# One written order for the keys' stage and cross-attention, ACT's too, with queries two units ahead throughout and feed-forward tiles between the last two units' work

## The chip, the cores and the metric

The kernel runs on one core of a Trainium2 chip. The core has a matrix engine (TensorE, PE in the profile, with its weight loads as PEld), a vector engine (VectorE, DVE), an activation engine (ScalarE, ACT), GpSimd (POOL) and a queue that issues most transfers (SyncE, SP). The metric is the device time of one execution in microseconds; lower is better. All arithmetic is in float32.

## What is computed

One decoder layer for 32 sequences of 64 tokens (2048 tokens) of width 512. `x` is replaced three times:

```python
x = _layernorm(x + _L0_attn_ref(x, ...))      # 32 heads of 128, 8 key heads, 512 cached keys + 64 new ones
x = _layernorm(x + _L0_xattn_ref(x, ctx_4096, Wq, bq, Wkv, bkv, Wo, bo))
x = _layernorm(x + _L0_ffn_ref(x, W, b, A, B, p_scores))

# cross-attention: 32 heads in 8 groups of 4; every sequence has 64 context rows of its own
q = (query @ Wq + bq);  k_, v_ = split(kv @ Wkv + bkv)
o = softmax(q k^T / sqrt(128)) v;   return o @ Wo + bo

# feed-forward: a full product and one of low rank (8 x 16), clamped by their norms
z = x W^T + b;  m = sum_e p_e (x A_e) B_e
return z + min(0.5 |z| / (|m| + 1e-6), 1) * m
```

## The kernel before

Tokens are handled in four blocks of 512 (tb 0 to 3), each of four tiles of 128 rows. `acc[tb]` holds a block's running x, rows on partitions. Large products are done by Strassen and Winograd's scheme with seven products in place of eight: each needs sums of its operands beforehand (by GpSimd mostly), and after each product its PSUM bank is read by VectorE or ACT and added up. Queries are done so on two levels (`DeepQueries`): sets s = 0 and s = 1, each with products 1 to 7. Few banks are at hand, so TensorE waits at a product whose bank has not been read yet.

There are four stages.

- **Self-attention**, to about 1820 us. The diff does not touch it.
- **The keys' stage** (`with ExitStack() as st`, L1244 to L1339): keys and values of the context, 15 pairs (gp, tb) of seven products each, the 16th having been done earlier (`KV_ORDER` 1, 6, 5, 7, 2, 4, 3; "step" counts them from pair (0, 1) on). Product 1 and 2 go to a bank that ACT reads (L591, L592), the others to banks that VectorE reads (L595). Between the products a table, `fill`, places other work at given steps: the first layernorm of blocks 1, 2, 3, 0. Of each block it places the statistics (`stats`, bn_stats on VectorE and a square root on ACT), the scaling by ACT (`scale_by_act`, L190: reciprocal and shift on VectorE, four pieces on ACT), four turns (`turn_rows`, L150) and 16 small transfers on SP (`move_rows`, L155) that together transpose the block, then `token_parts` (L1203): the operand sums of the block's tokens, which are stored to `tl_all` for all later queries. These sums are made by `deep_parts` (L413): ACT copies four inner blocks, r11, r21, r12 and r22, and GpSimd makes the sums; r12 is overwritten by GpSimd before ACT copies it.
- **Cross-attention** in 32 units n = (g, tb), g the key group. In the loop (L1572 to L1711), unit n does: `attend(n-1)` (weights by values, then `output_sums` on GpSimd into `sox`), `scores(n)`, the softmax of n (`largest`, `exponentials`, `denominators`, `weights`, `turn`, `move`), the queries of a later unit m (14 products), and the output product of unit n-1 (seven products `w`, added to `acc`). `prep` is the preparation of the next group's weights (`weight_parts`, on GpSimd), done after `q_sums` of units with m % 4 = 3. m is n + 2 up to n = 25; at n = 26 there are no queries (`SKIP`), from 27 to 30 m is n + 1, and 31 has none. As a block's last unit ends, its second layernorm is made (`projected`), with turns and moves into xT for blocks 0 and 1, and TensorE transposes for blocks 2 and 3.
- **Feed-forward** (`feed_forward`, L1503) of each block: `pu` (x by A), and for each tile `pz` (x by W) and `pm`. Blocks 0 and 1 come within the last units; blocks 2 and 3 after them.

What sets the order: a scheduler orders the instructions of each engine, except where an engine is put under `tc.manual_schedule`; then its instructions run in the order in which the program writes them. Before, the keys' stage has PE, DVE and Pool written and ACT by the scheduler; units 0 to 30 have PE, Pool, DVE and ACT written; from unit 31 on only PE and Pool. The queues (SP's above all) issue in the order they are given. In the trace each engine runs its instructions one behind the other, so a waiting instruction holds all that stand behind it.

```python
for k, tb in enumerate((1, 2, 3, 0)):
    stats, scale = layernorm_parts(tb, "a", by_act=True)
    i = place(17 * k, stats, True)
    i = place(i + 1, scale) + 1
    for j in range(TPB):
        i = place(i, lambda tb=tb, j=j: turn_rows(acc[tb][:, j, :], room, j))
    fill[i - 1].append(lambda: move_rows(room, raw0))
    fill.setdefault(i + 5, []).append(lambda tb=tb: all_parts(token_parts(tb, raw0)))
```

Of the kernel before, what the change touches and what calls it, by code (L numbers as in the profile page):

```python
# [16 lines left out]
P = 128  # L17
DIM = 512
# [34 lines left out]
def decoder_layer(  # L53
# [115 lines left out]
    def layernorm_parts(tb, name, by_act=False):  # L169
# [20 lines left out]
        def scale_by_act():  # L190
            nc.vector.reciprocal(rstd, rstd)
            shift = small.tile([P, TPB], F32, tag="shift", name=f"shift_{name}_{tb}")
            nc.vector.scalar_tensor_tensor(shift, mv[:, :, 0], -1.0, rstd, ALU.mult, ALU.mult)
            for j in range(TPB):
                nc.scalar.activation(
                    a[:, j, :], a[:, j, :], AF.Identity, bias=shift[:, j : j + 1],
                    scale=rstd[:, j : j + 1],
                )

        return stats, scale_by_act if by_act else scale  # L200
# [105 lines left out]
    def output_sums(o, name, fourth_last=True):  # L306

        a = {(i, j): o[j][:, :, i * HF : (i + 1) * HF] for i in range(2) for j in range(2)}
        t = {i: big.tile([P, 2, HF], F32, tag=f"so{i}", name=f"{name}_{i}") for i in range(1, 5)}
# [860 lines left out]
    with ExitStack() as ph:  # L1170
# [72 lines left out]

        with ExitStack() as st:  # L1244
            ke = st.enter_context(tc.tile_pool(name="ke", bufs=1))
            psum.append(st.enter_context(tc.tile_pool(name="kps", bufs=1, space=PSUM)))
            st.enter_context(tc.manual_schedule(engines={
                mybir.EngineType.PE, mybir.EngineType.DVE, mybir.EngineType.Pool
            }))
# [21 lines left out]
            fill = {}  # L1271
# [8 lines left out]
            for k, tb in enumerate((1, 2, 3, 0)):  # L1280
                stats, scale = layernorm_parts(tb, "a", by_act=True)
                i = place(17 * k, stats, True)
                i = place(i + 1, scale) + 1
                for j in range(TPB):
                    i = place(i, lambda tb=tb, j=j: turn_rows(acc[tb][:, j, :], room, j))
                fill[i - 1].append(lambda: move_rows(room, raw0))
                fill.setdefault(i + 5, []).append(
                    lambda tb=tb: all_parts(token_parts(tb, raw0))
                )
                for j in (0, 2):  # L1290
                    while i in fill:
                        i += 1
                    fill[i] = [lambda tb=tb, j=j: add_bias(tb, j)]

            def queries(n, p):
# [3 lines left out]
                for s in range(2):  # L1299
                    for group in ((1, 5), (6, 2), (7,), (3, 4)):  # L1300
                        for i in group:
                            q.step(s, i)
                            q.read()
                        if i == 4:
                            run(q.post(s))
                            next_operands(n + 1, s)
                        yield
# [3 lines left out]
            for k, (gp, tb) in enumerate(pairs):  # L1311
# [6 lines left out]
                for i in KV_ORDER:  # L1318
# [4 lines left out]
                    run(fill.pop(step, []))  # L1323
                    step += 1
# [6 lines left out]
                if tb == NTB - 1 and gp == 2:  # L1331
                    load_xq(0, raw0)
                    all_parts(weight_parts(raw0))
# [4 lines left out]
            assert not fill  # L1338
            psum.pop()  # L1339

        sb = ph.enter_context(tc.tile_pool(name="xa", bufs=2))
        d_2 = sb.tile([P, 7, 4, P], F32, name="d_2", bufs=1)
# [28 lines left out]
        def exponentials(n, pr):  # L1371
# [3 lines left out]
            es[pr] = e = sb.tile(shape, F32, tag="e", name=f"ex{g}_{tb}_{pr}")  # L1375
# [39 lines left out]
        def attend(n):  # L1415

            g, tb = units[n]
            oTs[n] = output_tiles(f"oTx{g}_{tb}")
# [35 lines left out]
            left = output_sums(oTs.pop(n), f"sox{g}_{tb}", False)  # L1454
# [4 lines left out]
        def projected(n):  # L1459
            g, tb = units[n]  # L1460
            del pjs[n]
            if g == NKV - 1:
                stats, scale = layernorm_parts(tb, "x", by_act=True)
                due.append(stats)
                scales.append(scale)
                xT.append((raw, wqs.rearrange(flat)[:, : NC * TB].rearrange(
                    "p (c n) -> p c n", c=NC), rooms[:, 0, :, :], rooms[:, 1, :, :])[tb])
                if tb < 2:
                    later.append(lambda: turn_block(tb))
                else:  # L1470
                    later.append(lambda: transpose_block(tb, "x2", FREE))

        def turn_block(tb):
            room = sb.tile([P, DIM // SQ, SQ, TPB], F32, tag="room", name=f"room2_{tb}", bufs=1)
            for j in range(TPB):
                turns.append(lambda j=j: turn_rows(acc[tb][:, j, :], room, j))
            turns.append(lambda: move_rows(room, xT[tb]))

        def a_turn():

            if turns:
                turns.pop(0)()
                if len(turns) == 1:
                    turns.pop(0)()

# [17 lines left out]
        def feed_forward(tb, between=None):  # L1503
# [3 lines left out]
            pu = sc.tile([P, TB], F32, tag="sc", name=f"pu{tb}")  # L1507
# [6 lines left out]
            for i in range(TPB):  # L1514
                if between and i == TPB - 1:
                    between()
# [4 lines left out]
                pz = bank([P, DIM], f"pz{u}", (("qx", "qz") * 2 if tb < 2 else FREE)[i])  # L1521
                pm = (sc.tile([P, DIM], F32, tag="sc", name=f"pm{u}") if tb < 2 or i % 2 else
                      bank([P, DIM], f"pm{u}", ("qy", "wz")[i // 2]))
                for c in range(NC):
# [3 lines left out]
                    if c == (NC - 1 if i == 0 else 1):  # L1528
# [18 lines left out]
        FREE = ("qx", "qz", "wx", "wy")  # L1547
        ffn_w, turns = [], []
        N = len(units)
        load_kv(0)  # L1550

        units_order = ExitStack()
        units_order.enter_context(tc.manual_schedule(engines={
            mybir.EngineType.PE, mybir.EngineType.Pool, mybir.EngineType.DVE,
            mybir.EngineType.Activation,
        }))


        def parts(n, *made):

            for part, pr in made:
                if n < N:
                    part(n, pr)

        due, prep, shifts = [], [], []
        mxs, es, dens, scales = {}, {}, {}, []

        LAST = N - 1  # L1570
        SKIP = N - NTB - 2
        for n in range(N + 1):  # L1572
            if n == LAST:

                units_order.close()
                ph.enter_context(tc.manual_schedule(
                    engines={mybir.EngineType.PE, mybir.EngineType.Pool}
                ))
            m = n + 2 if n < SKIP else n + 1 if SKIP < n < LAST else None
            if m:  # L1580
                qn = deep_queries(m, QS if n else [QS[0], {"x": "wx", "z": "wz", "w": "wy"}])

            def q_step(s, *products):
                for i in products if m else ():
# [3 lines left out]
            def q_sums(s):  # L1588
                if not m:
                    return  # L1590
                if s:
                    own = qn.post(s)
                    if m == n + 1:
                        shifts.extend(own)
                    run(shifts)
                    if m > n + 1:
                        shifts.extend(own)
# [6 lines left out]
            def w(i):  # L1604
                if n == 0:
                    return
                pj = pjs[n - 1]
                pj.step(i)
                pj.reads.pop(0)()
                if i == 4:  # L1610
                    projected(n - 1)

            def w_rest():
                if n:
                    pjs[n - 1].read()

            if n > 1:
                attend(n - 1)
            if n == N:
                run(scales)  # L1620
                run(later)
                feed_forward(1)
            elif n != 1:
                scores(n)
            parts(n, (largest, 0), (largest, 1))
            q_step(0, 1)
            if n == 0:
                load_xo(0)
                run(held)
            parts(n, (exponentials, 0), (exponentials, 1))  # L1630
            if n == LAST:
                load_ffn()
                norm = [*due, *scales, *later]
                due, scales, later = [], [], []
            if n == 0:
# [3 lines left out]
                parts(n, (weights, 0))  # L1639
                q_step(1, 1, 5)  # L1640
                parts(n, (weights, 1))
                q_step(0, 3, 4)
                q_sums(0)
                parts(n, (turn, 0), (turn, 1))
                move(n)
                q_step(1, 6, 2, 7)
# [4 lines left out]
            if m and m % NTB == NTB - 1 and m // NTB + 1 < NKV:  # L1651
# [5 lines left out]
            if not m:  # L1657
                run(shifts)
            if n == 1:
                attend(0)  # L1660
                q_step(0, 3, 4)
                q_sums(0)
                q_step(1, 1, 5)
                w(1)
                w_rest()
                q_step(1, 6)
            else:
                w(1)
                q_step(0, 3)
                w_rest()  # L1670
# [3 lines left out]
            parts(n, (weights, 1), (turn, 0))  # L1674
            w(2)
            parts(n, (turn, 1))
            if n < N:
                move(n)
            if n < LAST:
                run(due)  # L1680
            if n > 1:
                q_step(1, 6)
            q_step(1, 2, 7)
            w(6)
            q_step(1, 3, 4)
            q_sums(1)
            if n < LAST:
                run(scales)
                run(later)
            w(5)  # L1690
            a_turn()
            w(7)
            a_turn()
            w(3)
            a_turn()
            w(4)
            a_turn()
            if n < N and units[n][1] == 0:
                load_xo(units[n][0])
            if m and m % NTB == 0 and 1 < m // NTB + 1 < NKV:  # L1700
# [61 lines left out]
```

## Time and profile before

| what | value |
|---|---|
| median of 3 runs | 3049.51 us (3049.48 to 3049.62) |
| the profiled execution's own time | 3048.54 us |
| its span, first to last instruction | 3046.8 us |
| mean granted TensorE clock | 0.994 |
| TensorE busy | 2994.2 us, 16128 products |
| TensorE's gaps over 0.06 us, all | 41.9 us |
| of these before 100 us / 1780 to 2052 / 2052 to 2110 / from 2760 on | 8.2 / 7.5 / 5.8 / 19.9 us |

The profiled execution lies 0.97 us under the median, and 1.74 us of it lie around the span. The profile's page gives for each engine the busy time; a view of waits gives, for each engine, the idle time ahead of its instructions and what ended it ("PE qx_3x L479 <- ACT d_in L492" is a product into bank qx_3x by the instruction of line 479 that could start once ACT had finished the instruction of line 492 that writes d_in). A view of windows gives the busy time of each engine between two times and the clock that TensorE was granted (1.00 is full). A timeline gives instructions in order, with the wait ahead of each in brackets.

The stretches in which TensorE was granted half its clock begin at 2058.06 us (for 3.41 us), 2768.03 (6.83), 2884.09 (6.83), 2901.15 (3.41), 2948.94 (6.83), 2979.66 (3.41) and, after TensorE's last product, 3041.1 (7.68).

### The profile page before, as it was taken

The numbers are of one execution on the slowest core, as the hardware profiler recorded it, in microseconds if no ns is written. First come the engines' busy times: TensorE is split into PE (matmuls) and PEld (weight loads), VectorE is DVE, ScalarE is ACT, GpSimd is POOL, SyncE is SP. The second block draws the span as 40 slices with busy tenths as digits, with TensorE's granted clock in tenths as the row PEclk, the third lists the DMA queues.
The fourth block names the chain that finished last, engine by engine and source line by source line (L and its number), as shares of the span: only waits on it lengthen the run. The fifth ranks groups of instructions, "written<-read, shape, count | busy, mean of one in ns | idle before, by whom it ended". The sixth has DMA issues, their size and how long they took to land.

```text
span 3046.8 us, 46458 instructions
## 1 busy us (share of the span) xinstructions
PE 2994.2 (98%) x16128; PEld 2344.6 (77%) x16128; DVE 2130.9 (70%) x3905; ACT 1131.5 (37%) x2794; POOL 1218.1 (40%) x1024
## 2 busy tenths in 40 slices
PE   8999999999999999999999999999999999999988
PEld 6777777777777777777777768998999999998864
DVE  6787777877877877877877756535666656666665
ACT  4322232332233232232232232325555545545453
POOL 4221321321321322322322135647667657756531
PEclk9999999999999999999999999999999999999999
DMA  6454444444445445444444355655544545553421
GB/s 183 128 131 126 113 111 124 113 111 127 109 117 128 105 117 132 102 120 129 102 117 120 85 133 196 241 205 192 170 171 169 195 168 172 179 171 127 138 72 39
DMA packets 221785, 418.16 MB, mean 137 GB/s; under 512 B 48176, under 2 KB 102960, under 8 KB 212592
## 3 DMA queue, kind: packets, MB, share of 16 engines
q1 hardware_dynamic: 206464, 387.26, 44.2%
q0 software_dynamic: 4304, 19.01, 1.8%
q10 hardware_dynamic: 10784, 8.92, 1.0%
q8 instruction: 130, 2.13, 0.3%
q14 instruction: 103, 0.84, 0.1%
HBM read 207.12 MB, written 33.82 MB: 79 GB/s over the span
## 4 chain that ended last, share of the span: by engine, by line
PE 91%; DVE 4%; ACT 2%; SPq 1%; DMA 1%; issue 1%; POOL 1%; DVEq 0%; ACTq 0%; POOLq 0%
PE po L871 16%; PE s L820 16%; PE pox L1430 2%; PE sx L1360 2%; PE qx_0x L479 2%; PE qx_3x L479 2%; PE qx_1x L479 2%; PE qx_2x L479 2%; PE wx_1y L340 1%; PE w_1y L340 1%; PE q_3y L340 1%; PE w_0y L340 1%; PE q_2y L340 1%; PE w_3y L340 1%; PE q_0y L340 1%; PE q_1y L340 1%
## 5 line engine op out<-in xcount | busy, mean ns | idle before, releaser
L828 ACT ACTIVATE p<-s,nmax 128x576 f32<-128x576 f32 x512 | 379.0, 740 | 1210.1 <-DVE nmax L825 1165.3
L820 PE MATMUL s<-kT,qT 128*128 128x288 f32 x2048 | 574.7, 406 | 0.5 <-ACT p L828 0.5
L871 PE MATMUL po<-pT,v 128*128 128x512 f32 (+1 forms) x1280 | 548.9, 602 | 3.0 <-DMA pT<-T 2.4
L820 PEld LDWEIGHTS s<-kT,qT 128*128 128x128 f32 x2048 | 387.7, 190 | 100.6 <-issue 18.7
L825 DVE TENSOR_REDUCE nmax<-s 128x1 f32<-128x576 f32 x512 | 383.5, 749 | 59.5 <-PE s L820 58.7
L851 DVE STREAM_TRANSPOSE T<-p 128x576 f32<-128x576 f32 x512 | 393.9, 769 | 12.7 <-ACT p L841 7.4
L871 PEld LDWEIGHTS po<-pT,v 128*128 128x128 f32 (+1 forms) x1280 | 213.5, 189 | 202.5 <-issue 172.5
L843 DVE TENSOR_SCALAR p<-p,den 128x576 f32<-128x576 f32 x488 | 301.4, 618 | 17.1
L311 POOL TENSOR_TENSOR so<-oT,oT 128x512 f32<-128x512 f32 x32 | 40.7, 1271 | 545.3 <-ACT oT L894 545.2
L837 DVE RECIPROCAL den<-den 128x1 f32<-128x1 f32 x512 | 83.9, 164 | 224.8 <-ACT p L828 210.4
L314 POOL TENSOR_TENSOR so<-oT 128x512 f32<-128x512 f32 x32 | 40.7, 1270 | 310.3 <-PE w_1y L340 92.8
L1387 ACT ACTIVATE ex<-ex,denx 128x64 f32<-128x64 f32 x512 | 129.1, 338 | 2.8 <-DVE denx L1382 2.8
L1449 ACT ACTIVATE oTx<-pox,bv 128x128 f32<-128x128 f32 x256 | 73.4, 490 | 134.4 <-PE pox L1430 134.4
L236 POOL TENSOR_TENSOR tx<-xT 128x512 f32<-128x512 f32 x31 | 40.6, 1310 | 199.1 <-PE q_3z L340 63.3
L311 POOL TENSOR_TENSOR sox<-oTx,oTx 128x512 f32<-128x512 f32 x32 | 40.6, 1269 | 161.6 <-DVE oTx L1451 155.6
L521 POOL TENSOR_TENSOR qTx<-d_in 128x512 f32<-128x512 f32 x68 | 85.1, 1273 | 44.1 <-ACT d_in L497 42.8
L828 ACT ACTIVATION_READ_ACCUMULATOR p<-s,nmax 128x1 f32 x512 | 98.7, 193 | 0.0
L528 ACT ACTIVATE qTx<-qTx,bq 128x512 f32<-128x512 f32 x128 | 82.5, 713 | 15.0 <-POOL qTx L521 15.0
L521 POOL TENSOR_TENSOR qTx<-d 128x512 f32<-128x512 f32 x60 | 75.1, 1272 | 25.9 <-ACT d L497 24.5
L1451 DVE TENSOR_SCALAR oTx<-pox,bv 128x128 f32<-128x128 f32 x256 | 72.9, 423 | 14.1 <-PE pox L1430 14.0
L1360 PEld LDWEIGHTS sx<-kv_room,qTx 128*64 128x64 f32 x2048 | 62.5, 138 | 12.2 <-issue 9.9
L894 ACT COPY oT<-po 128x512 f32<-128x512 f32 x128 | 68.2, 587 | 4.3 <-PE po L871 3.8
(566 smaller groups left out, 6236.8 us busy)
## 6 DMA issues: line engine op xcount, KB each, us to landing
pT<-T SPq DMA_DIRECT2D x1016, 80.0 KB
pT<-T SPq DMA_DIRECT2D x1008, 64.0 KB
xT<-tl SPq DMA_DIRECT2D x31, 1792.0 KB
tlb<-tl SPq DMA_DIRECT2D x31, 1344.0 KB
xT<-in_xT SPq DMA_DIRECT2D x123, 256.0 KB
kv_room<-kv SPq DMA_DIRECT2D x33, 512.0 KB
pTx<-Tx SPq DMA_DIRECT2D x256, 64.0 KB
kv<-c SPq DMA_DIRECT2D x30, 512.0 KB
```

Of the source, the lines that this page charges most:

```text
L340: nc.tensor.matmul(self.banks[b][:, m, :], self.left[i][:, k, m * P : (m + 1) * P], self.right[i][:, k, :], start=(first and m + k == 0), ...
L479: nc.tensor.matmul(o[:, j, :], self.left[s][:, j, LEFT[i], :], self.right[s][:, j, RIGHT[i], :], start=(first and j == 0), stop=(j == len( ...
L521: nc.gpsimd.tensor_tensor(self.q[:, :, i, :, v, :], x.rearrange("p (o u) n -> p o u n", o=2), y.rearrange("p (o u) n -> p o u n", o=2), AL ...
L820: nc.tensor.matmul(s[:, a, :HALF], qTs[n // REP][:, units[n][2], i * P : (i + 1) * P], kTs[g][:, a * HALF : (a + 1) * HALF], start=True, s ...
L825: nc.vector.tensor_reduce(nmax, s[:, :, :HALF], AX.XY, ALU.max, negate=True)
L828: nc.scalar.activation(p.rearrange("q (a k) -> q a k", a=2), s[:, :, :HALF], AF.Exp, bias=nmax, accum_out=den,)
L837: nc.vector.reciprocal(den, den)
L843: nc.vector.tensor_scalar(p, p, den, None, ALU.mult)
L851: nc.vector.transpose(Ts[n][:, :, i, :], ps_.pop((n, i)).rearrange("q (b k) -> q b k", k=SQ))
L871: nc.tensor.matmul(pos[n].rearrange("d (a q) -> d a q", a=NQD), vs[units[n][0]][rows, v, :], pTs[n // 2][rows, :, chunk, :], skip_group_ch ...
L1360: nc.tensor.matmul(s[b * SEQ : (b + 1) * SEQ, i * REP + h, :], qTs[n][:, h, pr * HF + c0 : pr * HF + c0 + SEQ], kvs[n][:, pr, 0, c0 : c0 + ...
L1387: nc.scalar.activation(e[:, k, :], e[:, k, :], AF.Copy, scale=den[:, k : k + 1])
```

## The change

1. One manual order, `units_order`, covers PE, Pool, DVE and ACT from the start of the keys' stage to the end of unit 30 (before: the keys' stage had its own without ACT).
2. `layernorm_parts(..., by_act=True)` gives the scaling as a head (reciprocal and shift) and four pieces. In the keys' stage the head is placed at the step after the statistics, the pieces two by two at steps with remainder 2 or 5 by 7 (table `scaling`), each pair followed by its turns; `token_parts` at the first such step from seven after the last turn on.
3. The weights' preparation for unit 0 is placed at pair (3, 0), product 2, and shifts of the first queries wait in `shifts` and run at pair (3, 3), product 5, or in unit 0.
4. The exponentials have two fixed tiles in place of a rotating tag.
5. Queries: m is n + 2 in all units up to 29, none in 30. Units 0 and 1 are written anew; in unit 1 the sums of set 0 (and `prep`) come before `attend(0)`.
6. Units 29, 30 and what follows are written out: the statistics of block 0 after output product 4 in unit 29; its pieces, turns and moves in unit 30; then the feed-forward of block 0 with `attend(30)` before its last tile, the scores and softmax of 31, the feed-forward of block 1 with `attend(31)` before its last tile, the output products of 30 and 31 in the order 1, 5, 6, 3, 7, 2, 4, with block 2's transposes between those of 31, then blocks 2 and 3. `load_ffn` (the feed-forward's weights: three transfers on SP, nine on GpSimd) moves from unit 31 to unit 30.
7. The last unit's outputs and sums use `d_in` and `d_2`; the banks of the feed-forward are given as arguments, and `pm` follows the whole `pz` in the last tile of blocks 0 and 1 too.

```diff
+        def head():
             nc.vector.reciprocal(rstd, rstd)
             nc.vector.scalar_tensor_tensor(shift, mv[:, :, 0], -1.0, rstd, ALU.mult, ALU.mult)
+        def piece(j):
+            nc.scalar.activation(a[:, j, :], a[:, j, :], AF.Identity, ...)
...
+        units_order.enter_context(tc.manual_schedule(engines={PE, Pool, DVE, Activation}))
         with ExitStack() as st:
-            st.enter_context(tc.manual_schedule(engines={PE, DVE, Pool}))
...
             for k, tb in enumerate((1, 2, 3, 0)):
-                stats, scale = layernorm_parts(tb, "a", by_act=True)
+                stats, (head, *pieces) = layernorm_parts(tb, "a", by_act=True)
                 i = place(17 * k, stats, True)
-                i = place(i + 1, scale) + 1
-                for j in range(TPB):
-                    i = place(i, lambda tb=tb, j=j: turn_rows(acc[tb][:, j, :], room, j))
-                fill[i - 1].append(lambda: move_rows(room, raw0))
-                fill.setdefault(i + 5, []).append(lambda tb=tb: all_parts(token_parts(tb, raw0)))
+                i = place(i, head)
+                j = 0
+                while j < TPB:
+                    while i % 7 not in (2, 5):
+                        i += 1
+                    scaling.setdefault(i, []).extend(pieces[j : j + 2])
+                    for jj in (j, j + 1):
+                        last = place(i + 1 + jj - j, lambda tb=tb, j=jj: turn_rows(...)) - 1
+                    i, j = i + 1, j + 2
+                fill[last].append(lambda: move_rows(room, raw0))
+                i = last + 7
+                while i % 7 not in (2, 5):
+                    i += 1
+                scaling.setdefault(i, []).append(lambda tb=tb: all_parts(token_parts(tb, raw0)))
...
                         if i == 4:
-                            run(q.post(s))
+                            shifts.extend(q.post(s))
...
                     run(fill.pop(step, []))
+                    run(scaling.pop(step, []))
+                    if gp == 3 and tb == 3 and i == 5:
+                        run(shifts)
+                    if gp == 3 and tb == 0 and i == 2:
+                        run(first)
+                        run(second)
...
+            if n == 1:
+                q_step(0, 3, 4)
+                q_sums(0)
+                attend(0)
+                q_step(1, 1, 5, 6)
+                parts(n, (weights, 1), (turn, 0))
+                q_step(1, 2)
+                w(0, 1)
+                q_step(1, 7, 4)
+                parts(n, (turn, 1))
+                move(n)
+                q_step(1, 3)
+                q_sums(1)
+                w(0, 2, 6, 5, 7, 3, 4)
...
+                if n == LAST - 2:
+                    q_step(1, 6)
+                    w(n - 1, 6, 5, 7, 3, 4)
+                    norms[0][0]()
+                    q_step(1, 2, 7, 3, 4)
+                    q_sums(1)
...
+        n = LAST - 1
+        attend(n - 1)
+        load_ffn()
+        scores(n)
+        head, *pieces = norms[0][1]
+        head()
+        run(pieces)
+        parts(n, (largest, 0), (largest, 1))
+        w(n - 1, 1)
+        parts(n, (exponentials, 0), (exponentials, 1))
+        turns, moves = turn_parts(0)
+        run(turns, 2)
+        w(n - 1, 5)
+        run(turns)
+        moves()
+        parts(n, (denominators, 0), (denominators, 1))
+        w(n - 1, 6)
+        run(shifts)
+        parts(n, (weights, 0))
+        w(n - 1, 3)
+        parts(n, (weights, 1), (turn, 0))
+        w(n - 1, 7)
+        parts(n, (turn, 1))
+        move(n)
+        w(n - 1, 2, 4)
+        units_order.close()
...
+        norm(1, True)
+        feed_forward(0, "sc", ZT, ("sc", "sc", "sc", "qy"), {3: [lambda: attend(LAST - 1)]})
+        n = LAST
+        scores(n)
+        for part in (largest, exponentials, denominators, weights, turn):
+            parts(n, (part, 0), (part, 1))
+        move(n)
+        feed_forward(1, "wx", ZT, ("wy", "sc", "sc", "sc"), {3: [lambda: attend(LAST)]})
+        w(LAST - 1, 1, 5, 6, 3, 7, 2, 4)
+        norm(2, False)
+        turned = [transpose_tile(2, j, ("wx", "wy", "wz", "qz")[j]) for j in range(TPB)]
+        w(LAST, 1, 5, 6, 3, 7)
+        run(turned, 2)
+        w(LAST, 2)
+        run(turned)
+        w(LAST, 4)
+        norm(3, False)
+        feed_forward(2, "sc", ("wx", "wz", "wx", "wz"), ("sc",) * TPB, {
+            3: [transpose_tile(3, j, ("qx", "qz", "wy", "qy")[j]) for j in range(TPB)]
+        })
+        feed_forward(3, "sc", ("qx", "qz", "wx", "wz"), ("sc",) * TPB)
```

## The prediction

> **What bounds the kernel now.** I read the page first, then TensorE's waits by stage, then the stages' windows, then the timelines around the waits.
>
> ```profile
> PE 2994.2 (98%) x16128; PEld 2344.6 (77%) x16128; DVE 2130.9 (70%) x3905; ACT 1131.5 (37%) x2794; POOL 1218.1 (40%) x1024
> PE 91%; DVE 4%; ACT 2%; SPq 1%; DMA 1%; issue 1%; POOL 1%; DVEq 0%; ACTq 0%; POOLq 0%
> ```
>
> TensorE (PE) is busy 98% of the span and carries 91% of the chain that ended last. The change removes no product, so it can only move TensorE's idle gaps. The windows (start:end and length, then busy time of PE, PEld, DVE, ACT and POOL, the granted clock, the DMA share, GB/s) show where those are:
>
> ```profile
> 1840.00:2052.00 212.00, 206.38 (x1459) 193.97 (x1459) 109.11 (x163) 65.10 (x148) 116.99 (x99) 1.00 0.58 212
> 2052.00:2107.00 55.00, 49.22 (x479) 45.31 (x476) 30.69 (x60) 32.04 (x85) 40.53 (x33) 0.97 0.63 214
> 2107.00:2760.00 653.00, 653.00 (x5525) 596.62 (x5526) 405.39 (x756) 342.29 (x927) 441.54 (x357) 1.00 0.51 175
> ```
>
> Units 2 to 25 (2107 to 2760) have no gap at all. What can be won or lost lies in three places: the keys' stage (5.6 us of gaps), units 0 and 1 (5.8 us) and the tail from unit 26 on, whose waits are:
>
> ```profile
> PE qx_3x L479 <- ACT d_in L492: 4.0, 1, 4.0
> PE wx_1x L340 <- DVE acc L547: 3.6, 1, 3.6
> PE x L142 <- ACT oTx L1449: 3.1, 1, 3.1
> PE wx_3x L340 <- DVE acc L547: 2.6, 1, 2.6
> PE wx_1y L340 <- DVE acc L539: 2.3, 1, 2.3
> PE wx_2x L340 <- DVE acc L547: 2.3, 1, 2.3
> ```
>
> With four short ones (0.8, 0.6, 0.3, 0.3) they sum to 19.9 us. A longer gap also costs clock. TensorE's timeline behind the 3.6 us wait (start, busy, instruction, wait before):
>
> ```profile
> 2768.91 3.78 PE L340 MATMUL wx_1x<-xwo,oTx 128*128 128x256 f32 x8 [3.56 <-DVE acc L547]
> 2772.49 3.12 PE L340 MATMUL wx_1y<-xwo,sox 128*128 128x256 f32 x8
> 2775.44 0.81 PE L340 MATMUL wx_1z<-xwo,sox 128*128 128x256 f32 x3
> ```
>
> Products that start 1.73 us apart elsewhere start 3.58 and 2.95 apart here: the granted clock is 0.5 from 2768.03 for 6.83 us, and about 3.0 us are lost behind the wait itself. In this trace waits of 3.06, 3.56 and 4.05 us drew 6.83 us at 0.5 (about 3 lost each), those of 2.34, 2.60 and 2.68 us drew 3.41 (about 1.5 each), and those up to 2.30 drew none, nor did one of 2.45 at 66.5 us. I price a new wait so: over 3.5 us, 3 more; 2.3 to 3.5, where the trace has none, 1.5 and 3, 1.5 more; shorter, nothing. The tail of today holds 19.9 + 3 x 3 + 2 x 1.5 = 31.9 us.
>
> [...]
>
> **The change, part by part.**
>
> *Keys' stage, ACT in written order.* One product is 1.76 us on TensorE, and its bank is free only when VectorE or ACT has read it. ACT has waits here that cost little today:
>
> ```profile
> 1868.70 0.62 ACT L450 COPY tlb<-kv_room 128x512 f32<-128x512 f32 x1 [1.95 <-DMA kv_room<-d_in]
> 1873.98 0.62 ACT L450 COPY tlb<-kv_room 128x512 f32<-128x512 f32 x1 [4.67 <-POOL kv_room L422]
> 1874.51 0.47 ACT L591 ACTIVATE c<-kv_3x,bk 128x256 f32<-128x256 f32 x1
> ```
>
> The second line waits 4.67 us for GpSimd, which overwrites r12 only after three operations of 1.3 us; bank reads stand behind it. Four such waits make 18.8 us of ACT's time. The scheduler ran other copies first. Now the order is fixed: the four copies of the token sums stand together, and behind them two pieces of the layernorm scaling and the next pair's bank reads; the turns that wait for pieces stand ahead of VectorE's reads.
> - Head (reciprocal, shift) of block 1 now stands ahead of a bank read of product 5. Today that read starts at 1845.63 and TensorE follows at 1846.45 after 0.68 us. The square root ends at 1845.95, the reciprocal takes 0.17, the shift 0.64 to 1.01: the read starts near 1847.1, the wait grows by 1.4.
> - Block 1's token sums: the last two turns now stand behind the reads of step 10 (counted from pair (0,1)), and end about 3.8 us after step 11 starts, at 1862.1 (step 11 is today at 1857.07, plus the 1.4 above less 0.2). Moves land 13.1 us after their first issue (1855.5 to 1868.6 today): 1875.2; GpSimd's r12 is ready 5.2 later (1868.76 to 1873.95): 1880.4. Copies 1.2, first piece 0.8, two turns 2.2: the bank read starts at 1884.6, TensorE 0.8 later at 1885.4, where it would be at 1881.1. Wait 4.3, today 0.85: +3.4, and clock +3.
> - Block 2: its copies again hold ACT, with the next square root behind them; the wait comes out at 2.1 if the half clock behind block 1 lets ACT catch up, and at 4.3 if not; I take 2.8, today 1.42: +1.4, and clock +1.5.
> - Block 3: the copies fall where no bank read is due: today's 0.85 goes. Block 0: 1.6, today 0.07: +1.5.
> - Queries' last shifts come earlier (at product 5 of pair (3,3)): the wait of the first scores for ACT, 1.7, goes.
>
> Sum +1.4 +3.4 +3 +1.4 +1.5 -0.85 +1.5 -1.7 = +9.7. Bounds: -5.6 (all gaps go) to +13 (block 2 at 4.3, with 3 of clock).
>
> *Units 0 and 1.* Unit 0's first wait (2.68, ACT's copy d) stays: d takes room that the keys' tiles leave, whose last stores must land first. Rearranged products save about 0.6 in unit 0. In unit 1 the sums of set 0 and the preparation of weights now stand ahead of attend(0) on GpSimd. Today:
>
> ```profile
> 2083.26 1.27 POOL L311 TENSOR_TENSOR sox<-oTx,oTx 128x512 f32<-128x512 f32 x1 [5.97 <-ACT oTx L1449]
> 2093.68 2.50 POOL L422 TENSOR_TENSOR wq<-tx 128x512 f32<-128x512 f32 x2
> 2098.84 5.35 POOL L422 TENSOR_TENSOR wq<-wq 128x512 f32<-128x512 f32 x4
> ```
>
> The output sums (sox, 4 x 1.3) run first, the preparation (eight operations, 10.4 us) after. Afterwards the preparation runs about 2083.9 to 2094.3, and the second sox is there at 2096.9. The output product 6 that reads it is reached at 2093.7: wait 3.2. With shorter waits for banks (four of 0.35 to 1.5) against today's 0.88 and 1.25, unit 1 ends at 2105.7 instead of 2100.78: +4.9, saving of unit 0 included; clock +1.5. Sum +6.4; bounds 0 (GpSimd starts early enough) to +9.
>
> *Units 2 to 28.* Same order, 27.4 us each; moving queries one unit ahead from 26 on takes work from one unit to another. It fills unit 26, so its 3.56 goes (counted in the tail). The fixed tiles for the exponentials replace two rotating ones: nothing, bounds -1 and +1 by one exponential (0.63) a unit's start.
>
> *Tail.* New waits, from the start of unit 29 (about 2841.7) on:
> - Unit 29: the stats of block 0 stand between the output products and queries 2, 7, 3, 4. ACT's bank copy of product 7 queues behind a square root that waits for four bn_stats (0.8 each). This is today's 4.0 us wait in the same arrangement: 2884.84 square root, 2884.95 copy, 2885.46 TensorE. One product less stands between, so 5.1 (bounds 2.5 to 6.5); clock +3.
> - Scores of 30 wait for ACT's query shifts behind it: 1.0.
> - Unit 30 has no queries, so output products follow each other each 1.73 us while VectorE does softmax, two turns (1.06 to 1.10 each) and adds (0.69 and 1.21). Products 3 and 7 wait for adds behind these: 2.9 and 2.5 (bounds 0 and the 3.6 of unit 26, which has no queries today); they are one product apart, so clock +1.5 once.
> - First tile of the feed-forward: turns of block 0 end about 47.5 us after unit 29's start, the moves land 13.1 to 13.3 later at 60.8, TensorE is there at 54.9: wait 5.9 (bounds 0 and 8), clock +3. The feed-forward weights are now issued a unit earlier (three transfers on SP ahead of these moves, nine on GpSimd, 4.4 us, with nothing urgent behind them).
> - attend(31) waits 0.5 for its moves behind output stores on SP. The last output products (order 1,5,6,3,7,2,4) and the transposes between them hide the old waits for acc and oTx.
>
> Sum 5.1 + 1.0 + 2.9 + 2.5 + 5.9 + 0.5 + 7.5 clock = 25.4 against 31.9: -6.5. Bounds: -25 (only 7 us of waits left) to +3.
>
> **Sum.** +9.7 + 6.4 - 6.5 = +9.6 on the profiled execution's 3048.54: 3058.1. The median of the runs is 0.97 above it, so 3059.
>
> **Rivals.**
> 1. *The tail wins* (0.28). GpSimd and the moves are ready when ACT and VectorE come to them, and unit 29's stats end before product 7. Then keys' and unit 1 cost 0 to +6 together and the tail gives 16 to 25: 3024 to 3043, say 3034. For it: ACT is busy 37%, GpSimd 40%, so there is slack on the mean; 31.9 us stand in the tail. Against: the 4.67 us waits are of order, not of load. It decides once the moves of block 0 land before TensorE reaches the feed-forward.
> 2. *Each wait halves the clock* (0.15). Four or more of the new waits exceed 3 us, each drawing 6.83 us at 0.5 (block 2, unit 1 and both of unit 30 at 3 instead of 1.5, and their waits at the upper bounds): 6 to 16 us more, 3065 to 3075, say 3070.
> 3. *It does not do what it says* (0.12): gaps are exchanged one for one and the clock with them. Keys' +5, units +3, tail -8: 3049.
>
> My forecast has 0.45, with 3049 to 3066 as its own range.
>
> **How the numbers follow.** About 0.2% (6 us) is what a measurement of this kernel can tell: faster is below 3043.4, slower above 3055.6. Faster: rival 1, 0.28. Same: rival 3 and 0.10 of my own case, 0.22. Slower: 0.35 of mine and rival 2, 0.50. The range that leaves out 2 in 10 cuts rival 1 in its upper half and rival 2 at its upper end: 3034 to 3074.
>
> **What would show it.** In the profile after: ACT's wait for kv_room on GpSimd with kv_0x reads behind it and a TensorE gap near 1881 of about 4 us; a gap before wx_0y in unit 1 with POOL sox as releaser; 653 us without gaps from 2107 on still there; qx_3x waiting for ACT d_in again in unit 29; pu waiting for a DMA into tx. I would be wrong if TensorE showed under 8 us of gaps from 1840 to 2110, or if pu started without a wait.

## The result, and the profile after

The changed kernel takes 3071.62 us (median of 4 runs, 3070.91 to 3074.53) against 3049.49 us for the kernel before in the same comparison: a ratio of 1.0076, with a 95% interval of 1.0059 to 1.0094. It is 22 us slower. Its profiled execution took 3071.48 us with a span of 3069.7 us and a mean clock of 0.991 (before 0.994). Its line numbers are a little higher than before for the same instruction (L422 is now L427, L479 is L484, L340 is L345).

The windows of the changed kernel, same times as in the prediction (busy of PE, PEld, DVE, ACT and POOL, then the granted clock):

```profile
1840.00:2052.00 212.00, 191.52 (x1298) 179.31 (x1297) 98.81 (x152) 58.48 (x138) 109.94 (x95) 0.96 0.54 199
2052.00:2107.00 55.00, 47.65 (x446) 44.54 (x444) 24.01 (x45) 26.73 (x66) 24.81 (x20) 0.94 0.50 172
2107.00:2760.00 653.00, 645.63 (x5455) 588.87 (x5454) 399.82 (x748) 336.75 (x914) 436.15 (x353) 0.99 0.51 173
```

In the first window TensorE is idle for 20.5 us where it was for 5.6, and the clock fell to 0.96. Units 0 and 1 now reach into the third window, whose only gap of note is theirs. TensorE's waits in the changed kernel (us in all, times, longest), up to 2120 us, then from 2120 us on (wx_0y is still unit 1, the rest is the tail):

```profile
PE kv_1y L583 <- DVE c L600: 12.3, 2, 10.4
PE kv_2y L583 <- DVE c L600: 3.5, 1, 3.5
PE kv_0y L583 <- DVE c L600: 2.7, 1, 2.7
...
PE wx_0y L345 <- POOL sox L317: 6.6, 1, 6.6
PE qx_3z L484 <- DVE d_in L492: 4.1, 1, 4.1
PE pu L1534 <- DMA tx<-room: 2.3, 1, 2.3
PE wx_1z L345 <- DVE acc L544: 2.2, 1, 2.2
```

Two waits stand out, 10.4 and 6.6 us, both before unit 2. The tail's waits sum to 13.5 us where they were 19.9.

Since TensorE sets the time, stage lengths say it best. They are worked out from three points in each profile: the starts of the first product of the keys' stage and of the first of attend(1), and the end of the last product. Each column is from one profiled execution, the ratio from all runs.

| | keys' stage and units 0, 1 | from attend(1) to the last product | ratio to the kernel before |
|---|---|---|---|
| before | 264.1 | 935.3 | 1 |
| changed | 297.3 | 924.4 | 1.0076 [1.0059, 1.0094] |
| e1 left sums late | 282.9 | 924.3 | 1.0025 [1.0015, 1.0035] |
| e2 preparation late | 286.9 | 924.3 | 1.0044 [1.0027, 1.0060] |
| e3 ACT free in the keys' stage | 289.8 | 925.4 | 1.0055 [1.0038, 1.0072] |
| e4 tail alone | 265.2 | 923.4 | 0.9970 [0.9960, 0.9980] |
| e5 both edits | 277.8 | 923.4 | 0.9994 [0.9984, 1.0003] |
| e6 queries two ahead alone | 266.8 | 926.2 | 0.9984 [0.9974, 0.9993] |
| e7 statistics late | 264.2 | 925.5 | 0.9971 [0.9959, 0.9982] |
| e8 copies late | 266.5 | 924.4 | 0.9980 [0.9970, 0.9989] |
| e9 scores first | 265.8 | 923.4 | 0.9970 [0.9960, 0.9981] |
| e10 combination | 264.4 | 925.2 | 0.9968 [0.9955, 0.9980] |
| e11 combination, scores first | 266.2 | 925.6 | 0.9974 [0.9965, 0.9984] |
| e12 turns first | 265.2 | 920.5 | 0.9956 [0.9940, 0.9973] |

The kernel before, e4, e6, e7, e9 and e12 have the same order in the first column and still differ by up to 2.7 us there; columns that differ by less are not told apart.

The change lost 33.3 us in the first column and won 10.9 in the second. The first part is 19.4 us in the keys' stage (233.4 us up to the first scores; before 214.0, with 1.05 us for the 16 of their 64 products that it had already done there taken off) and 13.9 in units 0 and 1. With the start 0.5 us later this makes 22.9, the difference of the spans.

### The profile page after: what moved, and what is told of

Same layout as the page of the kernel before. It is cut to its first block, busy times and chain, and to the rows that moved or that the text cites. A ratio compares the mean times of both kernels' runs of the same rounds, so it can differ in the third digit from the quotient of the medians.

```text
span 3069.7 us, 46475 instructions
## 1 busy us (share of the span) xinstructions
PE 2999.0 (98%) x16128; PEld 2348.7 (77%) x16128; DVE 2126.4 (69%) x3905; ACT 1134.0 (37%) x2796; POOL 1216.4 (40%) x1024
## 5 line engine op out<-in xcount | busy, mean ns | idle before, releaser
L830 DVE TENSOR_REDUCE nmax<-s 128x1 f32<-128x576 f32 x512 | 383.8, 750 | 60.8 <-PE s L825 60.5
L316 POOL TENSOR_TENSOR so<-oT,oT 128x512 f32<-128x512 f32 x32 | 40.7, 1273 | 543.4 <-ACT oT L899 543.4
L1411 ACT ACTIVATE exps<-exps,denx 128x64 f32<-128x64 f32 x512 | 129.2, 338 | 5.7 <-DVE denx L1406 5.7
L316 POOL TENSOR_TENSOR sox<-oTx,oTx 128x512 f32<-128x512 f32 x31 | 39.4, 1270 | 139.8 <-DVE oTx L1482 134.3
```

The source lines that it names most:

```text
L830: nc.vector.tensor_reduce(nmax, s[:, :, :HALF], AX.XY, ALU.max, negate=True)
L1411: nc.scalar.activation(e[:, k, :], e[:, k, :], AF.Copy, scale=den[:, k : k + 1])
```

## The 10.4 us wait, step by step

GpSimd's timeline in the changed kernel around block 3's token sums:

```profile
1945.62 1.26 POOL L233 TENSOR_TENSOR xwkv<-xwkv,xwkv 128x512 f32<-128x512 f32 x1 [24.51 <-DMA xwkv<-in_xwkv]
...
1950.88 2.48 POOL L427 TENSOR_TENSOR xT<-kv_room 128x512 f32<-128x512 f32 x2
...
1954.78 1.26 POOL L427 TENSOR_TENSOR kv_room<-kv_room,xT 128x512 f32<-128x512 f32 x1
```

The same in the kernel before:

```profile
1931.92 2.49 POOL L422 TENSOR_TENSOR xT<-kv_room 128x512 f32<-128x512 f32 x2 [15.29 <-DMA kv_room<-d_in]
...
1948.41 1.28 POOL L229 TENSOR_TENSOR xwkv<-xwkv,xwkv 128x512 f32<-128x512 f32 x1
```

Before, the token sums came first and the sums of the last key weights (xwkv) after them. The change places the token sums some steps later, into pair (2,0); the load of these weights and their sums are written at the end of pair (1,3), and so stand ahead now. GpSimd waits 24.5 us for the weights to land, with the token sums behind it, though ACT copies from the same tokens from 1937.4 us on. Then ACT:

```profile
1956.07 1.14 ACT L455 COPY tlb<-kv_room 128x512 f32<-128x512 f32 x2 [17.48 <-POOL kv_room L427]
1957.12 0.20 ACT L180 ACTIVATE rstd_a<-rstd_a 128x4 f32<-128x4 f32 x1
1957.22 0.46 ACT L596 ACTIVATE c<-kv_0x,bk 128x256 f32<-128x256 f32 x1
```

ACT's copy of r12 waits 17.5 us for GpSimd. Behind it stand the next square root, which VectorE's head waits for, and a bank's read (kv_0x). VectorE's bank reads stand behind the head, and TensorE behind these. VectorE's reciprocal (the start of the head) and TensorE's product:

```profile
1957.35 0.18 DVE L193 RECIPROCAL rstd_a<-rstd_a 128x4 f32<-128x4 f32 x1 [10.44 <-ACT rstd_a L180]
```

```profile
1962.33 2.08 PE L583 MATMUL kv_1y<-te,wq 128*128 128x256 f32 x4 [10.43 <-DVE c L600]
```

One late load passes through three engines in fixed order.

## The experiments

The edits are shown shortened: `...` stands for lines left out, and some lines are summed up in a comment. A kernel before was run beside every group of experiments; the ratios are to that one.

**e1: the left sums behind the token sums.**

```diff
-                    kvw[gp + 2] = load_kv_left(gp + 2, ("wq", "wo")[gp])
+                    kvw[gp + 2], loads, sums = kv_left_parts(gp + 2, ("wq", "wo")[gp])
+                    run(loads)                 # sums at once for gp 2; for gp 3
+                    left_late.append(sums)     # after block 3's token_parts
```

> The changed kernel with one edit: GpSimd's sums of the last key weights (gp 3), which wait for a load, run behind block 3's token sums instead of ahead of them. Theory (a late step put ahead in a fixed order): the 10.4 us wait at kv_1y goes to under 1 us and its half clock with it, so 12 to 14 us less than the changed kernel: 3058 to 3060. Rival (ACT's written order itself holds the bank reads, whatever GpSimd does first): r12 still comes late for ACT, half the wait or more stays: 3065 to 3072.

Measured: 3057.65 us, 14.0 under the changed kernel. TensorE's waits in its keys' stage:

```profile
PE kv_0y L583 <- DVE c L600: 2.7, 1, 2.7
PE kv_2y L583 <- DVE c L600: 2.6, 1, 2.6
```

The 10.4 us wait is gone. Of the others block 1's two stand as they were (1.8 and 2.7), block 2's fell from 3.5 to 2.6, and block 0's grew from 0.5 to 1.8. ACT's order was the same, so the rival falls: for this wait, what GpSimd does first decides.

**e2: unit 1's preparation behind attend(0)'s sums.**

```diff
                 q_step(0, 3, 4)
-                q_sums(0)
+                q_sums(0)            # without the first part of prep
                 attend(0)
+                run(held_prep[0])    # that part; the rest of prep stays where it was
```

> The changed kernel with one edit: in unit 1 the preparation of the next weights (8 operations, 10.4 us on GpSimd) is run after attend(0)'s output sums instead of ahead of them. Theory: the 6.6 us wait of wx_0y for sox goes, with 2 to 3 us of half clock: 3062 to 3064. Rival (sox is late because its own inputs from ACT and VectorE are, or the preparation now makes unit 2 wait): 3068 to 3073.

Measured: 3062.78 us, 8.8 less; in the profile units 0 and 1 take 51.8 us from the first scores instead of 63.9. GpSimd in the changed kernel, then in this one (L427 is the preparation, L316 and L317 are the first two output sums):

```profile
2110.07 2.50 POOL L427 TENSOR_TENSOR wq<-tx 128x512 f32<-128x512 f32 x2
...
2121.83 1.26 POOL L317 TENSOR_TENSOR sox<-sox,oTx 128x512 f32<-128x512 f32 x1
```

```profile
2110.06 1.27 POOL L317 TENSOR_TENSOR sox<-sox,oTx 128x512 f32<-128x512 f32 x1
...
2113.87 2.50 POOL L427 TENSOR_TENSOR wq<-tx 128x512 f32<-128x512 f32 x2
```

The sums come 11.8 us earlier, the preparation 3.8 later (each on its profile's own scale; attend(0) starts 1.3 us earlier in the second), the wait at wx_0y is gone, and nothing waits for the preparation in unit 2. The theory holds. Units 0 and 1 are 12.1 us shorter in this profile, more than the 8.8 us between the medians, in part because block 3's wait, which the edit leaves alone, was longer in this execution (13.1 us for 10.4).

**e3: ACT by the scheduler in the keys' stage.**

```diff
-        units_order.enter_context(...)            # ahead of the keys' stage
+            st.enter_context(tc.manual_schedule(engines={PE, DVE, Pool}))   # in it
+        units_order.enter_context(...)            # behind it
```

> The changed kernel with one edit: in the keys' stage ACT is ordered by the scheduler again, PE, VectorE and GpSimd stay as written by the change. Theory (the path goes from GpSimd's r12 through ACT's fixed order to the bank reads): GpSimd's r12 of block 3 is as late as before (near 1956 us), but reads no longer queue behind its copy, so the 10.4 us wait goes or falls under 4, and the waits of blocks 1 and 2 fall too: 3052 to 3062. Rival (ACT's order does not matter, GpSimd's and VectorE's do): 3068 to 3073.

Measured: 3066.05 us, only 5.6 less. Both texts missed. Two of TensorE's waits there:

```profile
PE kv_2y L583 <- DVE c L600: 4.0, 1, 4.0
PE kv_1x L583 <- ACT c L597: 3.0, 1, 3.0
```

The 10.4 us became 3.5 (0.5 at kv_1y and 3.0 at kv_1x): the scheduler put one copy of r12 between the two reads of kv_1x, and it still waits 4.6 us for GpSimd. Block 2's wait stayed (4.0 for 3.5), block 0's grew (2.5 for 0.5). So with GpSimd as late as in the changed kernel, freeing ACT wins 5.6 us where GpSimd's order (e1) wins 14.0: ACT's written order passes the lateness on, but undoing it alone is the smaller gain. What an order that knew of the late operand would win was not run here; e8 comes near it.

**e4: the tail alone.** The keys' stage and units 0 and 1 of the kernel before, all else of the changed one.

```diff
-                stats, (head, *pieces) = layernorm_parts(tb, "a", by_act=True)
+                stats, scale = layernorm_parts(tb, "a", by_act=True)    # and placed as before
...
-                            shifts.extend(q.post(s))
+                            run(q.post(s))
...
             if n == 1:
+                attend(0)
                 q_step(0, 3, 4)
                 q_sums(0)
-                attend(0)
...
```

> The kernel before in the keys' stage and in units 0 and 1, with the changed kernel's units 2 to 31 and feed-forward (queries two units ahead to the last, tail written out). Theory (losses and gains are separate stages that add up): from attend(1) to the last product the changed kernel took 924.4 us against 935.3, so 10.9 us less than the kernel before: 3037 to 3040. Rival (the tail's gain hangs on its late start, for instance on loads that had more time): 3045 to 3050.

Measured: ratio 0.9970, 3039.80 us; the tail column is 923.4 us. The theory holds: the stages are separate, and the tail's gain does not need the late start.

**e5: e1 and e2 together.**

> The changed kernel with the edits of the first two experiments together (sums of the last key weights behind block 3's token sums; unit 1's preparation behind attend(0)'s sums). Theory (two separate waits in two stages): the savings of 14.0 and 8.8 us add up, 3047 to 3050, no difference to the kernel before: what the keys' stage still loses is what the tail wins. Rival (one saving contains part of the other, through the shift of the loads): 3052 to 3057.

Measured: ratio 0.9994. The savings of e1 (0.0051) and e2 (0.0032) add up to 0.0083, and the ratio fell by 0.0082. The theory holds: the two waits are separate.

**e6: the kernel before, with queries two units ahead.**

```diff
-        SKIP = N - NTB - 2
+        SKIP = N - 2
```

> The kernel before with one edit: queries two units ahead up to unit 29, so that unit 26 has queries and unit 30 has none; all else as before, the tail's order too. Theory (the tail's gain is in the written-out order; a unit without queries costs its waits wherever it is, and only moves from 26 to 30): 3047 to 3051. Rival (the gain is unit 26's 3.6 us wait and its half clock, which nothing pays back): 3042 to 3045.

Measured: 3041.55 us beside 3047.70 of the kernel before, ratio 0.9984 (0.9974 to 0.9993). The rival's 3042 to 3045 was meant against 3049.5, and by the ratio it holds. But the reason was neither text's. Its waits from 2700 us on:

```profile
PE wx_1x L340 <- DVE acc L547: 3.6, 1, 3.6
PE wx_2x L340 <- DVE acc L547: 3.1, 1, 3.1
```

The 3.6 us wait of a unit without queries moved from 2768.9 to 2879.5 us, as the theory had it. What went is the 4.0 us wait of qx_3x for ACT: that product belonged to unit 31's queries, which before ran in unit 30, behind block 0's square root; two units ahead they are done by then. By the second column this one edit has 9.1 of e4's 11.9 us; but the first column, which it does not touch, came out 2.7 longer in the same execution, and by the ratios it has 0.0016 of 0.0030. So half of the tail's gain or more comes from these queries alone. What the written-out order adds to it is not shown apart: the two intervals overlap (0.9974 to 0.9993 and 0.9960 to 0.9980).

**e7: e4 with unit 29's statistics behind its queries.**

```diff
-                    norms[0][0]()
                     q_step(1, 2, 7, 3, 4)
+                    norms[0][0]()
                     q_sums(1)
```

> The kernel of the fourth experiment (tail alone, 3039.8) with one edit: in unit 29 block 0's statistics stand behind the queries' products 2, 7, 3, 4 of set 1, not ahead of them. Theory (the square root that waits for the statistics holds ACT's bank copy): the 4.05 us wait at qx_3z goes with about 3 us of half clock, and the turns of block 0 do not come later since they wait for the scores of unit 30: 3033 to 3036. Rival (the statistics set when the turns and the moves into tx are done): the wait moves to pu, which grows by 7 to 10 us: 3039 to 3044.

Measured: ratio 0.9971, the same as e4. TensorE's waits:

```profile
PE pu L1519 <- DMA tx<-room: 4.3, 1, 4.3
PE sx L1369 <- ACT qTx L533: 3.9, 2, 3.7
```

The theory failed. The wait at qx_3z fell from 4.05 to 1.16 us, but the square root now stood ahead of the query shifts, so the scores of unit 30 waited 3.7 us for them, and pu 2 us more for its moves. The wait came back further on, in part at pu, where the rival said.

**e8: e5 with ACT's copies of r12 and r22 (and what follows them) three or four products later.**

```diff
-                scaling.setdefault(i, []).append(lambda tb=tb: all_parts(token_parts(tb, raw0)))
+                scaling.setdefault(i, []).append(early)    # first, and r21's copy
+                scaling.setdefault(late, []).append(lambda made=made: run(made))   # next place
```

> The kernel of the fifth experiment with one edit more: of the token sums in the keys' stage, ACT's copies of r12 and r22 (and the sums and the store behind them) stand three or four products later, behind the pieces and the bank reads that they held up. Theory (ACT's copy that waits for GpSimd holds the pieces, and these the turns and the bank reads): the waits of 2.7 (block 1) and 2.1 to 3.5 us (block 2) fall below 0.5 each, with their half clock 5 to 9 us less than the fifth experiment. Rival (the bank reads are late through VectorE's turns and the head, the copies only stand beside): within 1.5 us of the fifth experiment.

Measured: 3041.30 us, 5.4 under e5 (ratios 0.9980 and 0.9994); the keys' stage takes 214.7 us in the profile, 224.4 in e5. Its waits:

```profile
PE kv_2y L583 <- DVE c L600: 2.5, 2, 1.5
PE kv_0y L583 <- DVE c L600: 0.9, 1, 0.9
```

Block 1's wait fell from 2.6 in e5 to 0.9, block 2's from 2.2 to 1.5, and block 0's 3.0 went. The theory holds, except that a rest of 0.9 to 1.5 us stays, as in the kernel before. With this the keys' stage costs what it did before (214.0), and of the 33.3 us that the changed kernel lost in the first column the three edits together have given back 30.8.

**e9: e4 with the scores of unit 31 ahead of the first feed-forward tile.**

```diff
+        scores(LAST)                      # its keys loaded behind attend(29)
         feed_forward(0, ...)              # into other banks
-        scores(LAST)
```

> The kernel of the fourth experiment (tail alone) with one edit: the scores of unit 31 (2.1 us of TensorE, with its keys loaded a unit earlier and other banks for the feed-forward) stand ahead of the first feed-forward tile, where TensorE waits 2.35 us for block 0's moves. Theory (the moves set the end of that wait, work that is ready can fill it): pu's wait falls under 0.5 and about 2 us are saved, with up to 1.5 of half clock: ratio to the kernel before 0.9960 to 0.9966. Rival (the scores themselves wait for the last queries' shifts, or the moves slip with them): 0.9970 or more.

Measured: ratio 0.9970: nothing. The moves slipped: their first issue came 48.7 us behind the start of attend(28), where it was 47.7 in e4, and pu started at 61.2 for 59.6, with a wait of 4.0 us for them in place of 2.3. attend(30) now waits 3.0 us for VectorE. The rival holds, by its second reason; why the moves came later is not shown.

**e10 and e11: candidates.** e10 is e8's keys' stage with the old units 0 and 1 and the new tail; e11 adds e9's edit. Against e8:

```diff
             if n == 1:
+                attend(0)
                 q_step(0, 3, 4)
                 q_sums(0)
-                attend(0)
...
+        scores(LAST)                      # e11 alone, with e9's other lines
         feed_forward(0, ...)
```

> The changed kernel's keys' stage as mended in the eighth experiment (sums of the last key weights and ACT's copies of r12 and r22 later), the kernel before's units 0 and 1, and the changed kernel's tail: a candidate. Theory (keys' stage now equals the kernel before's, unit 0 and 1 in the old order save 1 to 2 us against the eighth): as the fourth experiment or up to 2 us under it, ratio 0.9963 to 0.9972. Rival (what the keys' stage saved by moving the first scores comes back as a wait of unit 0): 0.9978 or more.

> The candidate of the tenth experiment with the ninth's edit (scores of unit 31 ahead of the first feed-forward tile). Theory (they lie in different stages): the savings add up, ratio 0.9955 to 0.9967. Rival: the same as the better of the two.

Measured: 0.9968 and 0.9974. Neither can be told from e4; e11's sum of savings did not come.

**e12: e4 with block 0's turns and moves ahead of unit 30's softmax.**

```diff
+        turns, moves = turn_parts(0); run(turns); moves()
         parts(n, (largest, 0), (largest, 1))
         w(n - 1, 1)
         parts(n, (exponentials, 0), (exponentials, 1))
-        turns, moves = turn_parts(0); run(turns, 2)
         w(n - 1, 5)
-        run(turns); moves()
```

> The kernel of the fourth experiment (tail alone) with one edit: in unit 30 block 0's four turns and the moves stand ahead of the softmax's maxima and exponentials, so that the turns end near 2888.5 instead of 2893.1 us on the profile's scale. Theory (the moves into tx, 13 us after the last turn, set when the feed-forward starts): pu's wait of 2.35 us goes, and with up to 1.5 of half clock 2 to 4 us are saved: ratio to the kernel before 0.9957 to 0.9964. Rival (VectorE's later reads of the output products cost TensorE as much in unit 30): 0.9967 to 0.9985.

Measured: 3036.27 us, ratio 0.9956, and 920.5 us in the second column. Its waits from 2840 us on have no pu:

```profile
PE wx_1z L345 <- DVE acc L544: 3.1, 1, 3.1
...
PE pm L1538 <- DVE uT L1523: 1.6, 1, 1.6
```

The 2.3 us of pu went, and 1.4 us of wx_1y; wx_1z pays 0.9 and pm 1.1 of it back. The moves' first issue came 43.0 us behind the start of attend(28) and pu started at 56.4 without a wait. With e9 this says what bounds that place: the moves, not TensorE's lack of ready work. The theory holds. It has the lowest time of all, but its interval still holds e4's ratio.

## Why the prediction was right or wrong, point by point

The direction and the range held (3071.6 in 3034 to 3074). The size did not: 9.6 us were forecast, 22 came. That the range held is in part luck: its upper end came from the second rival's half clock, and what filled it was a wait that no text had. Without that wait e1 has 3057.7, near the 3059 of the forecast, but there too by cancelling: units 0 and 1 lost more than forecast and the tail won more.

- **Keys' stage, +9.7 forecast, +19.4 measured** (14.9 of waits, the rest the half clock). Head of block 1: +1.4 forecast, +1.2. Block 1: its chain was right in every step to about a microsecond (GpSimd starts at 1874.7, forecast 1875.2; the bank read at 1883.7, forecast 1884.6), and the wait is 2.7 for 4.3; the 3 us of clock did not come. Block 2: 3.5 for 2.8, with its 1.5 of clock. Block 0: 0.5 for 1.6. The wait of the first scores went, but the queries placed there wait 1.4 elsewhere. That ACT's copies, which wait for GpSimd, hold up the bank reads is shown by e8: 5.4 us.
- **The step that failed is "Block 3: the copies fall where no bank read is due: today's 0.85 goes".** It looked at ACT's place alone. The token sums had been moved past the sums of the last key weights in GpSimd's queue as well, and these wait for a load. The term was -0.85 us; the wait measured 10.4. e1 shows it: 14.0 of the 22 us.
- **Units 0 and 1, +6.4 forecast, +13.9 measured.** The mechanism and its place were right (product 6, wx_0y, waits for sox behind the preparation), the size was not: 6.6 for 3.2. I had the preparation start 9.8 us before TensorE reaches wx_0y; it starts 6.5 before, because the sums of set 0 ahead of it wait for products 3 and 4. e2 shows 8.8 us. That unit 0's 2.68 us wait stays was wrong: it is gone, but four waits of 0.9 to 1.4 stand there now, 4.9 us in all where there were 3.7.
- **Units 2 to 28, nothing**: right, no gap between 2134 and 2900.
- **Tail, -6.5 forecast, -10.9 measured.** Unit 29's wait 4.05 for 5.1 (at qx_3z, not qx_3x: VectorE's read of that bank stands behind the four bn_stats and then waits 0.2 us for ACT's copy), the scores of 30 none for 1.0, unit 30's 2.2 and 1.6 for 2.9 and 2.5, pu 2.3 for 5.9, attend(31) 1.9 for 0.5, the half clock 7.4 for 7.5. The mis-sized term is pu. Its moves came as forecast: pu starts 60.6 us after unit 29's first product, forecast 60.8. But TensorE was there only at 58.3, not at 54.9, so it had 3.4 us less to wait.
- **Rivals.** The first ("the tail wins") had the tail give 16 to 25 us; it gave 10.9, and 11.9 in e4, which has that tail alone and lands in the rival's range (3039.8). Its condition, that GpSimd is ready when ACT comes, did not hold in the keys' stage. Its upper end was also added up wrong: 6 lost and 16 won make 3039.5, not 3043. The second (half clock at each wait) had the time nearly right, 3070, for another reason: the half clock cost some 9 us more than before until unit 2 (half of the time at 0.5 in which TensorE ran), of which my forecast had 6, and one missed wait the rest. The third is excluded.

## What to carry to other kernels

Where an instruction is moved in a written order, look at what it passes in each of the queues that its parts are in; a wait for a load that was harmless at the end of GpSimd's list was dear ahead of what three other engines wait for (10.4 us of TensorE's time). Undo such moves one by one before a change is judged as a whole: here a tail worth 11 us was hidden under two misplaced steps worth 23 and a third (e8) worth 5. Where a transfer set the end here, taking away a wait ahead of it (e7, 0.9971) or filling the wait with other work (e9, 0.9970) won nothing over e4 (0.9970); making the transfer start earlier (e12) took the wait of 2.3 us at it away.

## What the runs showed of the hardware

In these profiles the half clock does not follow the length of a wait. The same wait of unit 0, in the kernel before and then in e4:

```profile
2058.06 2.08 PE L479 MATMUL qx_2x<-xT,wq 128*128 128x128 f32 x8 [2.68 <-ACT d L490]
```

```profile
2060.81 1.16 PE L484 MATMUL qx_2x<-xT,wq 128*128 128x128 f32 x8 [2.68 <-ACT d L495]
```

Both waited 2.68 us; the eight products behind it took 2.08 us in one and 1.16 in the other. In each of the 14 profiles all stretches at 0.5 begin on one grid of 3.413 us that runs through the kernel (within 0.001 us). I cut TensorE's gaps (those over 0.06 us, from 1780 us on) by that grid. At full clock, a step of the grid with 1.95 us or more of idle time was followed by half clock every time in these profiles, one with 1.67 or less never, and in between both were seen. In the kernel before the 2.68 us lay in one step; in e4 they lay across an edge (1.6 and 1.1). The 1.40 us wait at 2080.16 of the changed kernel drew half clock, with 0.5 us of another wait in the same step. So in these profiles the idle time within a step tells the half clock better than the length of a wait. It also places the 2.45 us wait at 66.5 us in the kernel before, which drew none: 0.6 us of it lay in one step and 1.9 in the next. My price list by length of wait in the prediction was the wrong form: block 1's 2.71 us wait, cut into 0.9 and 1.8, cost no clock.
